# The masked constant on VectorE, normalising passes in halves, scores one column block per slot

## The chip, the cores and the metric

The kernel runs on one core of a Trainium2 chip. A core has TensorE (matmuls into eight PSUM banks; PE in the profile, its weight loads PEld), VectorE (DVE), ScalarE (ACT), GpSimd (POOL), and SyncE (SP), which here issues the DMA transfers. The metric is device time in microseconds, the median of several executions.

## The reference, cut to what matters

Graph attention over 128 graphs of 128 nodes with 768 features, 12 heads of 64, in float32:

```python
h = jnp.maximum(_layernorm(x, axis=-1), 0.0)
q = split_heads(h @ Wq + bq); k = split_heads(h @ Wk + bk); v = split_heads(h @ Wv + bv)
scores = einsum('bhqd,bhkd->bhqk', q, k) / sqrt(64)
scores = scores + beta * adj[:, None]
scores = where(adj[:, None] > 0, scores, -9000000000000000.0)
probs = softmax(scores, axis=-1)
out = einsum('bhqk,bhkd->bhqd', probs, v)
x = x + merge_heads(out)
```

## The kernel before, in words

The graphs are taken in 32 groups G of four. A round of the main loop works on one group in three slices: `qk0` (queries and keys of the first six heads), `v` (values of all heads) and `qk1` (queries and keys of the other six). Every slice multiplies the same activations by other weights with a fast matrix product of fifteen block products in four chains. Each chain adds up in PSUM, and the sum is read out after each product that finishes something. So a later product of a chain has to wait until the earlier state has been read. One product is one **slot**; slots 0 to 14 run in the order `ZORDER`.

In `qk0` and `v` a product is once more cut into seven zones (`product_z`, matmuls L495), in two banks of four and three zones. Its activation operand needs four sums made by GpSimd (`inner`, L418 to L421), its weights come ready-made from DRAM as a tile `T` (L297, a ring of five). After the product its result goes to a tile of queries/keys or values. The first product that touches a tile **opens** it with copies: in `qk0` four by ScalarE (L514 to L517), in `v` two by VectorE with the bias (L508, L510) and two by ScalarE (L509, L511). Later products are added by VectorE (L521 for the first bank, L522 for the second). When a tile is whole, GpSimd recombines the zones (`decode`, L540 to L543 for queries and keys, L551 to L556 for values). In slice `qk0` slot 6 opens a tile from the two banks of chain a, and slot 8 is the next product of that chain; slice `v` is laid out alike. Slice `qk1` uses plain products (L571, L581, L587).

Into these slots other work is woven by the tables `todo`: a step under `at` is issued after the slot's matmuls and before its read-out, one under `(at, "post")` behind the read-out. Inside this region the order written is the order on each engine, so an engine that stands at one instruction holds up all that is queued behind it. The woven steps that matter here:

- `scores` (L609): the scores of column blocks of two heads, into two banks each; VectorE adds the bias tile and caps them (L613), ScalarE takes the exponential (L616). The first half of the heads is done in slots 1 and 2 of slice `v`: two column blocks (2, 0) in slot 1, the third (1) in slot 2.
- `norm` (L400): ReLU, scale and shift of a graph of the next group on ScalarE, four passes of 128x192 in place; slots 0, 2, 4 and 6 of slice `v`. `to_hT` (L406) transposes the result on VectorE.
- `bias_steps` (L436 to L449): makes the bias tile `biasT` of the next group, in slots 3, 5, 6 and 12 of slice `qk0`. In slot 5 GpSimd fills it with the masked constant (L439) and VectorE makes the predicate `kp` (L441) and the scaled adjacency (L442); in slot 6 VectorE copies the adjacency over the constant where the predicate says so (L444), and ScalarE squares the adjacency for a check of ranges (L445).
- `attend`: probabilities times values (L646), divided by the row sums (L623 to L630), added to the input by GpSimd (L656) and stored.

The first groups are handled by a separate start-up; rounds G = 2 to 30 have the bias steps in slice `qk0`, rounds G = 1 to 30 the normalising passes in slice `v`.

Of the kernel before, what the change touches and what calls it, by code (L numbers as in the profile page):

```python
# [19 lines left out]
GRP = 4  # L20
EPS = 1e-5
MASKED = -9000000000000000.0
# [92 lines left out]
def direct(ctx, tc, x, adj, wq, bq, wk, bk, wv, bv, beta, out, bad):  # L115
# [10 lines left out]
    nc = tc.nc  # L126
# [10 lines left out]
    NB = P // SQ  # L137
# [14 lines left out]
    def home_x(G, g):  # L152
        if not g % 2:
            xp[G, g // 2] = work.tile([P, 2 * NB, QD], F32, tag="x", name=f"x_{G}_{g}", bufs=2)
        t = xg[G, g] = xp[G, g // 2][:, (g % 2) * NB:(g % 2 + 1) * NB, :]
        return t
# [9 lines left out]
    for g in range(2):  # L166
        t = home_x(0, g)
# [158 lines left out]
    def moments_1(G, lo, hi):  # L326

        n = hi - lo
        bank = pm[G, lo, "bank"] = take()
        pm[G, lo] = bank[:, 0:4 * n].rearrange("p (s b h) -> p s b h", s=2, h=2)  # L330
        for q in range(0, P, HD):
            nc.tensor.matmul(pm[G, lo][q:q + HD, 0], mean8.rearrange("p a i -> p (a i)")[:, q:q + HD],
                             halves(G, lo, hi, 1), start=True, stop=True)
        mean = stat.tile([P, n], F32, tag="mean", name=f"mean_{G}_{lo}", bufs=2)
        nc.vector.tensor_reduce(mean, pm[G, lo][:, 0], AX.X, ALU.add)
        d = stat.tile([P, n, 2], F32, tag="dev", name=f"dev_{G}_{lo}", bufs=2)
        nc.vector.tensor_tensor(d, halves(G, lo, hi, 1), mean[:, :, None].to_broadcast([P, n, 2]), ALU.add)
        nc.vector.tensor_tensor(d, d, d, ALU.mult)
        nc.vector.scalar_tensor_tensor(d, halves(G, lo, hi, 2), 2.0 / QD, d, op0=ALU.mult, op1=ALU.add)
        return mean, d  # L340

    def moments_2(G, lo, hi, mean, d):

        n = hi - lo
        for q in range(0, P, HD):
            nc.tensor.matmul(pm[G, lo][q:q + HD, 1], mean8.rearrange("p a i -> p (a i)")[:, q:q + HD], d,
                             start=True, stop=True)
        ve = stat.tile([P, n], F32, tag="ve", name=f"ve_{G}_{lo}", bufs=2)
        nc.vector.tensor_reduce(ve, pm[G, lo][:, 1], AX.X, ALU.add)
        give(pm[G, lo, "bank"])  # L350
        nc.vector.tensor_scalar(ve, ve, -1.0, EPS, op0=ALU.mult, op1=ALU.add)
        r = stat.tile([P, n], F32, tag="rstd", name=f"rstd_{G}_{lo}", bufs=2)
        nc.gpsimd.tensor_tensor(r, ve, nhalf.to_broadcast([P, n]), ALU.pow)
        t = stat.tile([P, n], F32, tag="shift", name=f"shift_{G}_{lo}", bufs=2)
        shifted = nc.gpsimd.tensor_tensor(t, mean, r, ALU.mult)
        for b in range(lo, hi):
            rstd[G, b], shift[G, b] = r[:, b - lo:b - lo + 1], t[:, b - lo:b - lo + 1]
        return shifted
# [34 lines left out]
            for b in range(NB):  # L393
                rstd[G, g * NB + b], shift[G, g * NB + b] = to[:, b, 0, g:g + 1], to[:, b, 1, g:g + 1]

    def norm(G, g):
        for b in range(NB):
            t = xg[G, g][:, b, :]
            n = g * NB + b
            nc.scalar.activation(t, t, AF.Relu, bias=shift[G, n], scale=rstd[G, n])  # L400
# [32 lines left out]
    def bias_steps(G):  # L433

        a = turned[G] = work.tile([P, GRP, N], F32, tag="adjT", name=f"adjT_{G}", bufs=1)
        nc.vector.transpose(a, turned.pop((G, "raw")).rearrange("p g b j -> p g (b j)"))  # L436
        yield
        t = biasT[G] = work.tile([P, GRP, N], F32, tag="biasT", name=f"biasT_{G}", bufs=2)
        nc.gpsimd.memset(t, MASKED)  # L439
        kp = work.tile([P, GRP, N], U8, tag="kp", name=f"kp_{G}", bufs=1)  # L440
        nc.vector.tensor_scalar(kp, a, 0.0, None, op0=ALU.is_gt)  # L441
        nc.vector.tensor_scalar(a, a, beta_c, BIAS_CAP * ISCALE, op0=ALU.mult, op1=ALU.min)  # L442
        yield
        nc.vector.copy_predicated(t, kp, a)  # L444
        nc.scalar.activation(a, a, AF.Square, scale=1.0005 * math.sqrt(SUM_CAP) / (BIAS_CAP * ISCALE))  # L445
        yield
        bm = stat.tile([P, GRP], F32, tag="bm", name=f"bm_{G}", bufs=1)
        nc.vector.tensor_reduce(bm, a, AX.X, ALU.max)
        nc.vector.tensor_tensor(seen[:, 16:20], seen[:, 16:20], bm, ALU.max)  # L449
# [305 lines left out]
    def slice_of(G, sl, todo, order=range(len(PRODUCTS))):  # L755
        run([product(G, sl, n, order) for n in order], todo)

    def slice_z(G, sl, todo):
        run([product_z(G, sl, n) for n in ZORDER], todo)
# [167 lines left out]
    def then(at, f, *args):  # L927
        todo.setdefault(at, []).append(lambda: f(*args))

    def bias(G, *at):  # L930
        def go():
            if G not in steps:
                steps[G] = bias_steps(G)
            next(steps[G], None)
        for n in at:
            then(n, go)

    def attention(G, u, at):
        for i, j in enumerate((2, 0, 1)):
            then(at[i] - 3, load_xo, G, 3 * u + j)  # L940
            then((at[i], "post"), attend, G, 3 * u + j)

    def at_slots(f, G, slots):
        for at, names in slots:
            for name in names:
                then(at, f, G, *((int(name[1]), int(name[2])) if f is to_hT else (name,)))

    def activations(G):

        at_slots(to_hT, G, ((2, ("A10",)), (9, ("A12",))))  # L950
        at_slots(sum_acts, G, ((2, (0,)), (3, (2,)), (5, (3,)), (6, (4,)), (7, (5,)), (10, (1,)), (11, (6,)), (12, (7,)),
                               (13, (8,)), (14, (9,))))
        at_slots(inner, G, ((6, (0,)), (7, (4,)), (8, (2,)), (9, (1,)), (10, (8,)), (11, (6,)), (12, (5,)), (13, (3,)),
                            (14, (10,))))

    def rest_of_activations(G):
        at_slots(sum_acts, G, ((0, (10,)),))
        at_slots(inner, G, ((0, (7,)), (1, (13,)), (2, (9,)), (3, (11,)), (4, (12,)), (5, (14,))))
# [48 lines left out]
    for G in range(1, NG):  # L1007
        more = G + 1 < NG
        todo.clear()
        if G > 1:  # L1010
            rest_of_activations(G)
        else:
            at_slots(to_hT, 1, ((0, ("A00",)),))
            at_slots(sum_acts, 1, ((0, (2,)), (1, (5,)), (2, (4,)), (3, (8,)), (5, (9,))))
            at_slots(inner, 1, ((0, (2,)), (1, (6,)), (2, (5,)), (3, (10,)), (4, (7,)), (5, (13,)), (6, (9,)), (7, (14,))))
        for n, order in ((1, (2, 0)), (2, (1,))):
            then((n, "post"), scores, G - 1, 1, order)
        attention(G - 1, 1, AV_Z)
        if G == 1:
            bias(1, 0, 2, 3, 5)  # L1020
            for r in range(2):
                then(r, load_x, 2, r)
            for g in range(GRP):
                then(5 + 2 * g, stats, 2, g)
            then(6, add_raw, 2)
            then(13, lambda: mom.extend(moments_1(2, 0, GRP * NB)))
            then(14, lambda: moments_2(2, 0, GRP * NB, *mom[2:]))
        elif more:
            bias(G + 1, 3, 5, 6, 12)
        slice_z(G, "qk0", todo)  # L1030

        todo.clear()
        for n, order in ((1, (2, 0)), (2, (1,))):
            then((n, "post"), scores, G, 0, order)
        if more:
            for g in range(GRP):
                then((0, 2, 4, 6)[g], norm, G + 1, g)
            for name, at in (("A01", 4), ("A00", 5), ("A02", 6), ("A11", 9)):
                then(at, to_hT, G + 1, int(name[1]), int(name[2]))
            if G == 1:  # L1040
                bias(2, 8, 9, 10, 12)
                for at, n in enumerate((3, 4, 5, 6, 7, 8, 9, 10, 13, 14)):
                    then(at + 3, sum_weights, "qk1", n)
            if G + 2 < NG:
                then(13, load_halves, G + 2, 0)
        slice_z(G, "v", todo)
        if not more:
            break

        todo.clear()  # L1050
        attention(G, 0, AV_AT)
        activations(G + 1)
        if G + 2 < NG:
            for g, at in enumerate((2, 5, 8, 11)):
                then(at, row_stats, G + 2, g)
                if g < 3:
                    then(at, load_halves, G + 2, g + 1)
            for r, at in enumerate((6, 11)):
                then(at, load_x, G + 2, r)
            then(13, row_moments, G + 2)  # L1060
            then(14, add_raw, G + 2)
        slice_of(G, "qk1", todo)
# [154 lines left out]
```

## Time and profile before

| what | value |
|---|---|
| median of three runs | 2959.27 us (2958.37 to 2959.87) |
| the profiled execution's own time | 2957.3 us |
| its span | 2955.5 us |
| mean granted TensorE clock | 0.981 |
| DMA traffic | 660.88 MB, mean 224 GB/s |

A round takes 89.3 us in the trace. A line of a timeline gives the start and the length in us, the engine, the source line, the operation, what it writes and reads, its shapes, how many such instructions follow each other, and in brackets how long the engine was idle before it and for what it waited. An instruction may start before the one ahead of it on its engine has ended. A matmul of float32 shows as two records of 64 columns of weights. A line of the waits gives who waited, for whom, the total in us, how often, and the longest. A line of the windows gives the stretch, its length, the busy time and instructions of PE, PEld, DVE, ACT and POOL, the granted clock, the DMA share and GB/s.

### The profile page before, as it was taken

The numbers are of one execution on the slowest core, as the hardware profiler recorded it, in microseconds if no ns is written. First come the engines' busy times: TensorE is split into PE (matmuls) and PEld (weight loads), VectorE is DVE, ScalarE is ACT, GpSimd is POOL, SyncE is SP. The second block draws the span as 40 slices with busy tenths as digits, with TensorE's granted clock in tenths as the row PEclk, the third lists the DMA queues.
The fourth block names the chain that finished last, engine by engine and source line by source line (L and its number), as shares of the span: only waits on it lengthen the run. The fifth ranks groups of instructions, "written<-read, shape, count | busy, mean of one in ns | idle before, by whom it ended". The sixth has DMA issues, their size and how long they took to land.

```text
span 2955.5 us, 113446 instructions
## 1 busy us (share of the span) xinstructions
PE 2784.0 (94%) x46433; PEld 2431.7 (82%) x46433; DVE 2131.3 (72%) x4794; ACT 1351.1 (46%) x3999; POOL 2287.8 (77%) x4086
## 2 busy tenths in 40 slices
PE   7989999999999999999999999999999999999998
PEld 6778888888888888888888788888888887888887
DVE  3877777677777777777777776777777777767765
ACT  1435444445344444444454444444444544444443
POOL 2777878777877778887878877788877787777883
PEclk9999999999999999999999999999999999999999
DMA  9678777877777777778777777777787777777764
GB/s 216 196 236 232 217 218 229 244 236 215 219 236 219 248 230 217 218 226 247 235 221 215 233 220 246 232 213 226 224 244 236 218 216 230 225 242 230 212 193 130
DMA packets 526217, 660.88 MB, mean 224 GB/s; under 512 B 105460, under 2 KB 401664, under 8 KB 525696
## 3 DMA queue, kind: packets, MB, share of 16 engines
q1 hardware_dynamic: 525368, 653.20, 75.1%
q8 instruction: 368, 6.03, 0.8%
q14 instruction: 153, 1.25, 0.1%
q10 hardware_dynamic: 328, 0.40, 0.1%
HBM read 589.26 MB, written 64.21 MB: 221 GB/s over the span
## 4 chain that ended last, share of the span: by engine, by line


## 5 line engine op out<-in xcount | busy, mean ns | idle before, releaser
L495 PE MATMUL bank<-spbuf,T_qk 128*64 128x128 f32 x7440 | 673.3, 278 | 0.2 <-issue 0.2
L630 ACT ACTIVATE o<-bank,sm 128x64 f32<-128x64 f32 x1524 | 354.8, 315 | 667.9 <-DVE sm L624 522.8
L495 PE MATMUL bank<-T_v,spbuf 128*64 128x128 f32 x7440 | 647.8, 273 | 0.0
L646 PEld LDWEIGHTS bank<-v,e 128*64 128x64 f32 x6048 | 434.8, 144 | 107.5 <-ACT o L630 0.2
L495 PE MATMUL bank<-S,T_qk 128*64 128x128 f32 x4092 | 414.9, 282 | 109.7 <-ACT qk L515 106.3
L495 PEld LDWEIGHTS bank<-T_v,spbuf 128*64 128x64 f32 x7440 | 458.4, 137 | 0.3 <-ACT o L630 0.3
L646 PE MATMUL bank<-v,e 128*64 128x65 f32 x6048 | 449.4, 228 | 0.0
L495 PEld LDWEIGHTS bank<-spbuf,T_qk 128*64 128x64 f32 x7440 | 445.4, 141 | 0.5 <-issue 0.5
L495 PE MATMUL bank<-T_v,S 128*64 128x128 f32 x4092 | 402.8, 275 | 17.5 <-ACT v L509 15.6
L581 ACT ACTIVATE qk<-bank,bqk 128x256 f32<-128x256 f32 x372 | 156.7, 475 | 551.6 <-PE bank L571 422.0
L571 PE MATMUL bank<-S,wqk 128*64 128x256 f32 x2976 | 389.5, 380 | 0.0
L495 PEld LDWEIGHTS bank<-S,T_qk 128*64 128x64 f32 x4092 | 252.9, 142 | 127.0 <-ACT qk L515 113.5
L521 DVE TENSOR_TENSOR v<-v,bank 128x512 f32<-128x512 f32 x310 | 211.9, 684 | 150.4 <-PE bank L495 96.6
L571 PE MATMUL bank<-S,qk_T 128*64 128x256 f32 x2480 | 305.6, 379 | 0.0
L551 POOL TENSOR_TENSOR v<-v 128x128 f32<-128x128 f32 x186 | 86.0, 462 | 269.4 <-ACT x L400 145.2
L656 POOL TENSOR_TENSOR xo<-xo,o 128x512 f32<-128x512 f32 x189 | 242.7, 1284 | 57.0 <-ACT o L630 57.0
L613 DVE SCALAR_TENSOR_TENSOR e<-bank,biasT 128x512 f32<-128x512 f32 x378 | 237.4, 683 | 67.9 <-PE bank L609 67.7
L495 PEld LDWEIGHTS bank<-T_v,S 128*64 128x64 f32 x4092 | 257.1, 137 | 30.8 <-ACT v L509 23.3
L587 DVE TENSOR_TENSOR qk<-qk,bank 128x512 f32<-128x512 f32 (+1 forms) x311 | 208.2, 670 | 47.3 <-PE bank L571 34.0
L521 DVE TENSOR_TENSOR qk<-qk,bank 128x512 f32<-128x512 f32 x310 | 210.7, 680 | 42.8 <-ACT qk L515 22.7
L616 ACT ACTIVATE e<-e 128x512 f32<-128x512 f32 x378 | 227.3, 629 | 17.8 <-DVE e L613 17.3
L540 POOL TENSOR_TENSOR qk<-qk 128x256 f32<-128x256 f32 x186 | 135.7, 730 | 106.3 <-DVE qk L521 58.4
(164 smaller groups left out, 5883.2 us busy)
## 6 DMA issues: line engine op xcount, KB each, us to landing
T_qk<-kept_qk SPq DMA_DIRECT2D x465, 448.0 KB, 4.6
T_v<-kept_v SPq DMA_DIRECT2D x465, 448.0 KB, 4.9
x<-in_x_dram SPq DMA_DIRECT2D x254, 192.0 KB, 4.7
xo<-in_x_dram SPq DMA_DIRECT2D x189, 256.0 KB, 4.8
out_dram<-xo SPq DMA_DIRECT2D x189, 256.0 KB, 5.2
half<-in_x_dram SPq DMA_DIRECT2D x232, 192.0 KB, 4.0
adj<-in_adj_dram SPq DMA_DIRECT2D x128, 64.0 KB, 2.6
kept_qk<-prep_qk SPq DMA_DIRECT2D x15, 448.0 KB, 5.0
```

What stands on the lines that cost most here:

```text
L495: nc.tensor.matmul(p[z // 4][q:q + HD, z % 4, :], lhs[:, q:q + HD], rhs, start=(first and z % 4 == 0), stop=True, skip_group_check=True)
L521: nc.vector.tensor_tensor(t[:, 0:4], t[:, 0:4], p[0], op)
L540: e.tensor_tensor(t[:, 1:4:2], t[:, 1:4:2], twice(0), ALU.add)
L551: e.tensor_tensor(v[:, 0:2, 0:HD], heads(0), heads(3), ALU.add)
L571: nc.tensor.matmul(p[q:q + HD, i, :], lhs[:, q:q + HD], rhs, start=(first and i == 0 and c == 0), stop=(c == 1), skip_group_check=True)
L581: opened[0] = nc.scalar.activation(t[:, i, :], p[:, i, :], AF.Identity, bias=bqk[:, i, oc:oc + 1], scale=float(sign))
L587: added[G] = nc.vector.tensor_tensor(t[:, :, cols], t[:, :, cols], p[:, :, cols], ALU.add if sign > 0 else ALU.subtract)
L613: taken[0] = nc.vector.scalar_tensor_tensor(e, ps[oc, i].rearrange("p (g n) -> p g n", g=GRP), SCORE_CAP * ISCALE, biasT[G], op0=ALU.min, ...
L616: nc.scalar.activation(e, e, AF.Exp, scale=1.0 / ISCALE)
L630: nc.scalar.activation(o[:, b], pa[:, b, 0:HD], AF.Copy, scale=t[:, 1, b:b + 1])
L646: nc.tensor.matmul(pa[q:q + HD, 2 * g + i, :], es[G, oc, i][:, 2 * r + g, q:q + HD], vt[G, "v", r, h // 4][:, 4 * g + h % 4, :], start=Tru ...
L656: nc.gpsimd.tensor_add(t, t, o.rearrange("p a (b j) d -> p (a b) (j d)", j=2))
```

## The change

Three edits, which change no arithmetic:

1. The memset that fills `biasT` with the masked constant is issued to VectorE instead of GpSimd, at the same place in the program.
2. In slice `v` the four passes of the first two graphs' `norm` are issued in halves, two passes behind the read-out of each of slots 0 to 3; those of the third and fourth graph go to slots 4 and 5 (before the read-out, where they were in 4 and 6). Three of the transposes `to_hT` come one slot later.
3. The scores in slice `v` are done one column block in each of slots 1, 2 and 3, in the order 2, 0, 1.

```diff
-    def norm(G, g):
-        for b in range(NB):
+    def norm(G, g, lo=0, hi=NB):
+        for b in range(lo, hi):
             t = xg[G, g][:, b, :]
             n = g * NB + b
             nc.scalar.activation(t, t, AF.Relu, bias=shift[G, n], scale=rstd[G, n])
...
         t = biasT[G] = work.tile([P, GRP, N], F32, tag="biasT", name=f"biasT_{G}", bufs=2)
-        nc.gpsimd.memset(t, MASKED)
+        nc.vector.memset(t, MASKED)
...
         todo.clear()
-        for n, order in ((1, (2, 0)), (2, (1,))):
+        for n, order in ((1, (2,)), (2, (0,)), (3, (1,))):
             then((n, "post"), scores, G, 0, order)
         if more:
-            for g in range(GRP):
-                then((0, 2, 4, 6)[g], norm, G + 1, g)
-            for name, at in (("A01", 4), ("A00", 5), ("A02", 6), ("A11", 9)):
+            for g in range(2):
+                for h in range(2):
+                    then((2 * g + h, "post"), norm, G + 1, g, 2 * h, 2 * h + 2)
+            for g in range(2, GRP):
+                then(2 + g, norm, G + 1, g)
+            for name, at in (("A01", 5), ("A00", 6), ("A02", 7), ("A11", 9)):
                 then(at, to_hT, G + 1, int(name[1]), int(name[2]))
```

## The prediction

> **What bounds the kernel now.** I read the page's first section, then the page's groups, the waits sorted by total, and last the timelines of one round (one group of four graphs), engine by engine. The rounds repeat closely, so one stands for the rest.
>
> ```profile
> span 2955.5 us, 113446 instructions
> PE 2784.0 (94%) x46433; PEld 2431.7 (82%) x46433; DVE 2131.3 (72%) x4794; ACT 1351.1 (46%) x3999; POOL 2287.8 (77%) x4086
> ```
>
> TensorE is the bound, and only 2955.5 − 2784.0 = 171.5 us of its time is idle. Whoever wants to be faster without touching the matmuls has to find this idle time. The waits name it:
>
> ```profile
> ACT adjT L445 <- DVE biasT L444: 144.7, 31, 7.4
> DVE biasT L444 <- POOL biasT L439: 126.5, 29, 4.4
> PE bank L495 <- ACT qk L515: 106.3, 29, 3.7
> PE bank L495 <- ACT v L509: 15.6, 29, 1.1
> PE bank L609 <- POOL qk L543: 6.0, 19, 0.4
> ```
>
> The columns are who waited, for whom, us in total, times, longest. One wait, 29 times 3.67 us, holds 106.3 of the 171.5 us: matmuls of slice qk0 wait for an opening copy of ScalarE. The two lines above it occur as often and have the same size: ScalarE's L445 waits for VectorE's L444, which waits for GpSimd's memset L439. The timelines of GpSimd, VectorE, ScalarE and TensorE show whether they are one chain:
>
> ```profile
> 1425.26 0.53 POOL L439 MEMSET biasT<- 128x512 f32 x1
> 1427.27 0.73 POOL L540 TENSOR_TENSOR qk<-qk 128x256 f32<-128x256 f32 x1 [1.48 <-ACT adjT L445]
> ...
> 1420.22 0.65 DVE L441 TENSOR_SCALAR kp<-adjT 128x512 uint8<-128x512 f32 x1
> 1420.90 0.56 DVE L442 TENSOR_SCALAR adjT<-adjT,beta_c 128x512 f32<-128x512 f32 x1
> 1425.82 0.73 DVE L444 COPY_PREDICATED biasT<-kp,adjT 128x512 f32<-128x512 uint8 x1 [4.35 <-POOL biasT L439]
> ...
> 1421.49 0.36 ACT L517 ACTIVATE qk<-bank,bqk 128x128 f32<-128x128 f32 x1
> 1426.58 0.63 ACT L445 ACTIVATE adjT<-adjT 128x512 f32<-128x512 f32 x1 [4.73 <-DVE biasT L444]
> 1427.12 0.35 ACT L514 ACTIVATE qk<-bank,bqk 128x128 f32<-128x128 f32 x1
> 1427.37 0.48 ACT L515 ACTIVATE qk<-bank 128x384 f32<-128x384 f32 x1
> ...
> 1423.61 0.39 PE L495 MATMUL bank<-S,T_qk 128*64 128x128 f32 x4
> 1423.83 0.39 PE L495 MATMUL bank<-spbuf,T_qk 128*64 128x128 f32 x4
> 1427.90 0.44 PE L495 MATMUL bank<-S,T_qk 128*64 128x128 f32 x4 [3.69 <-ACT qk L515]
> ```
>
> They are. The memset stands in GpSimd's queue behind its zone sums and ends at 1425.79. VectorE had all else for L444 at 1421.46 and starts it at 1425.82, 0.03 us behind the memset. ScalarE stands 4.73 us at L445, and behind it in its queue are the copies L514 to L517 that empty slot 6's two banks. Slot 8 adds onto those banks, so TensorE starts it at 1427.90, 0.05 us after L515 ends, where the step between starts (1423.83 − 1423.61 = 0.22) would have given 1424.05. The hole is 3.85 us from start to start.
>
> **Part 1, the memset on VectorE.** It leaves GpSimd's queue and stands on VectorE ahead of L441. No row shows a VectorE memset of 128x512. Below it costs nothing but an issue; above, the 0.73 of L444, which reads two tiles and writes one of this size. I take 0.56, L442's row, one pass over the same shape. Then L441, L442 and L444 follow without a wait, and L444 starts at 1421.46 + 0.56 = 1422.02, 3.80 earlier. What is queued behind the memset on VectorE is only L441, L442 and L444 themselves. ScalarE is free from 1421.85 (end of L517), so L445 also comes 3.80 earlier, at 1422.78, L514 at 1423.32, and L515 ends at 1427.85 − 3.80 = 1424.05. Slot 8 could start at 1424.10, against 1424.05 by TensorE's own pace. So 0.05 us of the hole is left, 3.80 goes. With 0.73 it would leave 0.22, with nothing it would leave none and TensorE itself limits: the gain lies between 3.6 and 3.85 a round. 29 rounds give −110 us (−105 to −112).
>
> The Trainium skill prices it: "VectorE: DVE Perf Modes", section on zero memsets issued as uint32, has a memset take one cycle per element whatever the type, which at the page's 0.96 GHz is an estimated 0.53 us; the sum by that is less than 1 us away. No run here shows it yet.
>
> What is late next? GpSimd keeps its backlog of zone sums (the last ends at 1425.26, where the memset began, and belongs to slot 14, six products on) and then the decodes L540 to L543. These now start at 1425.26 rather than 1427.27, 2.0 us earlier where TensorE is 3.8 us earlier. At the end of that queue scores wait for L543 already (6.0 us over 19 times). Without idle GpSimd gains back the 1.48 us before L540 and smaller gaps, and in part 3 the third column's scores move one product later, so I put nothing for it; it costs up to 0.4 a round if that is wrong.
>
> **Part 2, V's opening copies and the normalising passes.** ScalarE is the tight engine in the first seven slots of slice v:
>
> ```profile
> 1442.81 1.86 ACT L400 ACTIVATE x<-x,block 128x192 f32<-128x192 f32 x4
> 1444.56 0.49 ACT L509 ACTIVATE v<-bank 128x384 f32<-128x384 f32 x1
> 1446.53 0.49 ACT L509 ACTIVATE v<-bank 128x384 f32<-128x384 f32 x1 [1.20 <-DVE v L508]
> 1447.27 2.42 ACT L616 ACTIVATE e<-e 128x512 f32<-128x512 f32 x4
> 1451.99 1.14 ACT L616 ACTIVATE e<-e 128x512 f32<-128x512 f32 x2
> 1457.91 0.48 ACT L509 ACTIVATE v<-bank 128x384 f32<-128x384 f32 x1
> ...
> 1443.09 0.28 DVE L508 TENSOR_TENSOR v<-bv_b,bank 128x128 f32<-128x128 f32 x1
> 1445.08 0.69 DVE L521 TENSOR_TENSOR v<-v,bank 128x512 f32<-128x512 f32 x1 [1.52 <-ACT v L509]
> 1446.55 2.48 DVE L613 SCALAR_TENSOR_TENSOR e<-bank,biasT 128x512 f32<-128x512 f32 x4
> ...
> 1444.61 1.98 PE L609 MATMUL bank<-qk 64*64 64x128 f32 x64
> 1446.52 0.44 PE L495 MATMUL bank<-T_v,S 128*64 128x128 f32 x4
> 1449.68 0.45 PE L609 MATMUL bank<-qk 64*64 64x128 f32 x8 [0.36 <-POOL qk L543]
> 1458.44 0.44 PE L495 MATMUL bank<-T_v,S 128*64 128x128 f32 x4 [0.52 <-ACT v L509]
> ```
>
> From 1442.81 to slot 6's copy at 1457.91 it runs through, but for 1.20 us; slot 8 waits for that copy (0.52). The change keeps every one of these instructions ahead of slot 6's copy: four graphs' passes, five pairs of copies, six exponentials. So it can only shift ScalarE's idle time. Four shifts. First, it starts with L509 instead of the norm, which waits for L508: 1443.09 + 0.28, and 0.10 for the signal, is 1443.47, +0.66. Second, L521 of slot 1, which stood 1.52 us for the late L509 (0.49 from 1444.56), needs L509 (now 1443.47 + 0.49 = 1443.96) and slot 1's matmuls, done at the latest when the scores start at 1444.61: it comes 0.5 to 1.0 us sooner, and with it slot 1's L508 and L509, at 1445.5 to 1446.0. ScalarE is ready for that at 1443.47 + 0.77 (a pair of copies: 1446.53 − 1.20 − 1444.56) + 0.93 (half a norm of 1.86) = 1445.17; its idle is 0.35 to 0.85 instead of 1.20, on the mean −0.6. Third, the first column's exponentials follow slot 1's copies at once, and their L613 starts only when that column's scores end: 0 to 0.3 of new idle, +0.15. Fourth, three pairs of exponentials (3 × 1.14) against four and two (2.42 + 1.14), −0.14. Together about +0.1 a round, with ends −0.5 (slot 8's wait of 0.52 gone) and +0.6 (the second shift does not come): over 30 rounds +3 us, from −15 to +18.
>
> **Part 3, one column of scores per slot.** Same matmuls (64 in 1446.52 − 1444.61 = 1.91, 0.96 a column), spread over three slots. It lets go the wait for L543 in the last column (0.36). But slot 8 is held by ScalarE, which isn't sooner, so TensorE just waits there longer: 0 us. Every L613 keeps its duration; VectorE and ScalarE get the pairs in the order that they had. Three transposes L406 come one slot later on VectorE, the first right behind the last half pass, ahead of slot 5's L508; they feed slice qk1, which starts nine slots on, and VectorE waits there for ScalarE as it does now: 0. No DMA, and no queue of GpSimd or SyncE, is moved by parts 2 and 3.
>
> **The sum.** 2957.3 us is the profiled execution's own time (span 2955.5), 2.0 below the median of the runs shown, 2959.27. 2957.3 − 110 + 3 = 2850; against the median 2852. About 0.2% (6 us) is what a measurement of this kernel can tell from no change.
>
> **Rivals.** *DMA becomes the next wait.* The hole was also time in which T tiles caught up:
>
> ```profile
> 1424.20:1427.90 3.70, 0.02 (x2) 0.00 (x0) 1.76 (x3) 1.32 (x4) 2.22 (x5) 1.00 1.04 359
> 1427.90:1441.40 13.50, 13.50 (x292) 13.50 (x294) 10.72 (x29) 5.13 (x22) 11.21 (x16) 1.00 0.75 232
> 1458.40:1469.20 10.80, 10.76 (x198) 10.76 (x199) 8.28 (x15) 0.26 (x1) 10.17 (x22) 1.00 0.88 307
> ```
>
> The last two columns are the DMA share and GB/s. 359 × 3.7 + 232 × 13.5 = 4.46 MB now pass in 17.2 us and must pass in 13.4. At 359 GB/s that takes 12.4 us and hides; at the 307 of the end of slice v, where products also follow each other without a hole and TensorE hardly waits, 14.5, 1.1 us a round too much: 29 × 1.1 = 32, so 2884. For it: DMA is full in the hole. Against it: five tiles of lead, and only the last bytes of the stage must be in time. 0.12. The Trainium skill, "DMA: Bandwidth & Descriptors", Specifications, gives some 358 GB/s as the limit of HBM for one core; the trace agrees (359), so there is little above the demand of 333 GB/s.
>
> *V's first slots cost more* (the upper end of part 2): 2867. 0.12.
>
> *Slower: V's slots 1 to 3 begin to alternate.* With one column per slot ScalarE might stand for each column's scores (0.96) and its first L613 (0.62 each of the 2.48), 1.58 three times, and 0.66 at the start, less the 1.20 there is now: 4.2 a round. Over 3.8 it eats part 1; here it would end at +0.4 × 30 = +12, 2971. It decides from the point at which ScalarE has emptied its queue before a column's scores end. Against it: ScalarE still owes two passes when the second and third columns arrive. 0.03.
>
> *The change doesn't do what it says*: L444 waits for something else that ends at the same time. 0.03 us after the memset, in 29 rounds, speaks against it. 2959, 0.04.
>
> **How the numbers follow.** Forecast 0.69 (2835 to 2867, parts 1 and 2 with their ends), DMA 0.12, V worse 0.12, none 0.04, slower 0.03. The range takes in the forecast's ends and reaches to the DMA case: 2835 to 2884. Faster 0.93, same 0.04, slower 0.03.
>
> **What would show it.** Right: the wait for L515 falls below 10 us in total, L444's wait for L439 is gone, the wait for L509 grows from 15.6 to some 30 or 40 us (the slots before it run undisturbed, ScalarE no faster), a VectorE memset of about 0.56 us appears 32 times. Wrong: matmuls L495 waiting for DMA T_qk by more than 10 us, waits for POOL L543 grown, or the wait for L509 above 60 us.

## The result and the profile after

| | median us | lowest to highest | ratio to before, 95% interval |
|---|---|---|---|
| before, beside it | 2959.57 | 2958.37 to 2961.78 | |
| after | 2828.45 | 2826.57 to 2829.16 | 0.9555 [0.9539, 0.9572] |

The change makes the kernel 131 us faster. Forecast were 2852 us, in a range that began at 2835. The sign holds, but the time is 23.5 us under the forecast and lies below the range.

The first section of the page after:

```profile
span 2827.0 us, 113416 instructions
PE 2753.4 (97%) x46433; PEld 2391.0 (85%) x46433; DVE 2187.4 (77%) x4826; ACT 1357.7 (48%) x3999; POOL 2293.8 (81%) x4054
```

TensorE's idle time went from 171.5 to 2827.0 − 2753.4 = 73.6 us, 97.9 less. But the span is 128.5 shorter: TensorE's *busy* time fell as well, by 30.6 us, with the same 46433 instructions. The prediction had looked for time in the idle part alone, and had taken the busy part as fixed.

Every ratio in this document is to the kernel before, run beside the kernel in question; the median of before was 2951.5 to 2959.6 us in the four batches of runs.

The waits after (who, for whom, us in total, times, longest), then the groups by line:

```profile
ACT adjT L445 <- DVE biasT L444: 32.2, 31, 7.7
PE bank L495 <- ACT v L509: 35.4, 30, 1.2
PE bank L495 <- DMA T_qk<-kept_qk: 3.6, 2, 3.0
PE bank L609 <- POOL qk L543: 0.7, 2, 0.4
```
```profile
L444 DVE COPY_PREDICATED biasT<-kp,adjT 128x512 f32<-128x512 uint8 x32 | 28.0, 874 | 1.0
L439 DVE MEMSET biasT<- 128x512 f32 x32 | 15.5, 485 | 1.8
L441 DVE TENSOR_SCALAR kp<-adjT 128x512 uint8<-128x512 f32 x32 | 11.6, 363 | 0.0
```

The wait for L515 (106.3 us) and L444's wait for L439 (126.5) are gone; the wait for L509 has grown from 15.6 to 35.4; DMA is no new wait. The same place as in the prediction's timelines, in one round of after, on VectorE, ScalarE and TensorE:

```profile
1363.35 0.55 DVE L522 TENSOR_TENSOR qk<-qk,bank 128x384 f32<-128x384 f32 x1
1363.96 0.48 DVE L439 MEMSET biasT<- 128x512 f32 x1
1364.36 0.36 DVE L441 TENSOR_SCALAR kp<-adjT 128x512 uint8<-128x512 f32 x1
1364.76 0.56 DVE L442 TENSOR_SCALAR adjT<-adjT,beta_c 128x512 f32<-128x512 f32 x1
1365.35 0.88 DVE L444 COPY_PREDICATED biasT<-kp,adjT 128x512 f32<-128x512 uint8 x1
...
1366.26 0.63 ACT L445 ACTIVATE adjT<-adjT 128x512 f32<-128x512 f32 x1 [0.81 <-DVE biasT L444]
1366.80 0.35 ACT L514 ACTIVATE qk<-bank,bqk 128x128 f32<-128x128 f32 x1
1367.05 0.48 ACT L515 ACTIVATE qk<-bank 128x384 f32<-128x384 f32 x1
...
1367.43 0.39 PE L495 MATMUL bank<-spbuf,T_qk 128*64 128x128 f32 x4
1367.65 0.39 PE L495 MATMUL bank<-S,T_qk 128*64 128x128 f32 x4
```

The four VectorE instructions follow each other without a wait. L515 ends at 1367.53, and slot 8 starts at 1367.65, 0.22 behind the matmuls before it: TensorE's own step, no hole.

**Where the other 30 us were.** What the prediction did not look at is the granted clock behind the hole of the kernel before. Windows of before, at a hole (1513.53 to 1517.22) of another round than the one that the prediction quotes; columns as there, the granted clock is the third number from the end:

```profile
1513.40:1517.20 3.80, 0.13 (x4) 0.00 (x0) 1.76 (x3) 1.30 (x4) 2.33 (x5) 1.00 1.02 360
1517.20:1520.70 3.50, 3.48 (x52) 3.48 (x54) 1.10 (x4) 1.33 (x6) 2.02 (x5) 0.62 0.25 91
```

Behind the quoted hole, at 1427.90, the same stretch looks like this, and in after, behind slot 8's start, like the second fence:

```profile
1427.90:1431.40 3.50, 3.50 (x79) 3.50 (x80) 1.79 (x7) 1.41 (x6) 2.50 (x5) 1.00 0.40 131
```
```profile
1367.60:1371.10 3.50, 3.50 (x84) 3.50 (x82) 2.65 (x7) 1.40 (x6) 3.34 (x7) 1.00 1.03 347
```

Busy is 3.48 to 3.50 us in all three, but 52 matmuls pass at a clock of 0.62 and 79 or 84 at full clock. The timeline of TensorE in before shows the switch inside it:

```profile
1517.60 0.39 PE L495 MATMUL bank<-spbuf,T_qk 128*64 128x128 f32 x4
...
1517.94 0.53 PE L495 MATMUL bank<-spbuf,T_qk 128*64 128x128 f32 x4
1518.25 0.44 PE L646 MATMUL bank<-v,e 128*64 128x65 f32 x4
1518.47 0.65 PE L495 MATMUL bank<-S,T_qk 128*64 128x128 f32 x4
```

Four matmuls of one form take 0.39, then 0.65 us. In the trace's record of the clock this is a stretch of 3.41 us at half clock, and it stands behind 22 of the 29 holes of before (behind one more it is 6.83 long). In after there is none in the rounds from G = 2 on. The mean times of a round's parts, worked out from the starts of the first matmuls of the slots, over the undisturbed middle of each trace, in us (before is split by the clock):

```
kernel                       rounds  qk0 0-8  qk0 8-end  v 0-2  v 2-8  v 8-end   qk1   round
before, full clock                5    19.32      13.55   5.06  11.91    10.84  28.70   89.38
before, 3.41 at half clock       21    19.31      15.12   5.06  11.39    10.75  28.70   90.32
before, all                      26    19.31      14.81   5.06  11.49    10.77  28.70   90.14
after                            26    15.47      13.69   4.19  12.95    10.75  28.70   85.75
memset_only                      27    15.49      13.68   5.89  11.41    10.79  28.70   85.96
without_memset                   26    19.30      16.27   4.19  12.94    10.75  28.70   92.15
columns_only                     26    19.27      14.43   4.19  12.37    10.75  28.70   89.70
memset_and_halves                25    15.47      13.65   5.90  12.66    10.75  28.70   87.14
memset_and_columns               26    15.47      13.67   4.20  12.79    10.75  28.70   85.58
late_by_4                        27    18.02      14.13   4.19  12.93    10.75  28.70   88.73
late_by_7                        26    19.79      15.81   4.19  12.93    10.75  28.70   92.17
late_by_10                       26    21.79      15.56   4.19  12.93    10.75  28.70   93.92
norms_behind_slot6               26    15.48      13.66   4.19  11.61    10.78  28.70   84.43
```

The half clock costs 15.12 − 13.55 = 1.57 us behind the hole, of which 0.52 come back in slice v (11.91 to 11.39, since ScalarE and GpSimd are less late there: slot 2, which stops for L543, takes 3.53 to 3.56 us in the rounds at full clock and 2.71 to 3.42 in the others), and 0.94 in the round. One of the five rounds at full clock lost 0.43 us for another reason at the end of slice `v`; the other four take 89.29, against which half clock costs 1.03 a round. The kernels below the first four lines are those of the experiments.

### The profile page after: what moved, and what is told of

It reads as the page before. It is cut to its first block, busy times and chain, and to the rows that moved or that the text cites. A ratio compares the mean times of both kernels' runs of the same rounds, so it can differ in the third digit from the quotient of the medians.

```text
span 2827.0 us, 113416 instructions
## 1 busy us (share of the span) xinstructions
PE 2753.4 (97%) x46433; PEld 2391.0 (85%) x46433; DVE 2187.4 (77%) x4826; ACT 1357.7 (48%) x3999; POOL 2293.8 (81%) x4054
## 4 chain that ended last, share of the span: by engine, by line
## 5 line engine op out<-in xcount | busy, mean ns | idle before, releaser
L495 PE MATMUL bank<-spbuf,T_qk 128*64 128x128 f32 x7440 | 658.7, 273 | 0.9 <-POOL qk L543 0.5
L646 PEld LDWEIGHTS bank<-v,e 128*64 128x64 f32 x6048 | 412.3, 137 | 110.6 <-ACT o L630 0.2
L495 PEld LDWEIGHTS bank<-spbuf,T_qk 128*64 128x64 f32 x7440 | 439.2, 137 | 1.4 <-POOL qk L543 0.8
L495 PE MATMUL bank<-T_v,S 128*64 128x128 f32 x4092 | 403.3, 274 | 36.0 <-ACT v L509 35.4
L646 PE MATMUL bank<-v,e 128*64 128x65 f32 x6048 | 433.8, 221 | 0.1
L495 PE MATMUL bank<-S,T_qk 128*64 128x128 f32 x4092 | 401.5, 274 | 4.2 <-DMA T_qk<-kept_qk 3.0
L613 DVE SCALAR_TENSOR_TENSOR e<-bank,biasT 128x512 f32<-128x512 f32 x378 | 240.5, 685 | 89.4 <-PE bank L609 89.3
L418 POOL TENSOR_TENSOR spbuf<-S 128x128 f32<-128x128 f32 x341 | 182.9, 537 | 44.1 <-DVE S L411 44.1
```

The lines of the kernel that those rows point to most:

```text
L418: e.tensor_tensor(t[:, 0], a[:, 0, N:H2], a[:, 1, N:H2], ALU.add)
L495: nc.tensor.matmul(p[z // 4][q:q + HD, z % 4, :], lhs[:, q:q + HD], rhs, start=(first and z % 4 == 0), stop=True, skip_group_check=True)
L613: taken[0] = nc.vector.scalar_tensor_tensor(e, ps[oc, i].rearrange("p (g n) -> p g n", g=GRP), SCORE_CAP * ISCALE, biasT[G], op0=ALU.min, ...
L646: nc.tensor.matmul(pa[q:q + HD, 2 * g + i, :], es[G, oc, i][:, 2 * r + g, q:q + HD], vt[G, "v", r, h // 4][:, 4 * g + h % 4, :], start=Tru ...
```

## The experiments

**One edit alone, and one undone.** The theory was that the memset is all of the gain; the rival, that parts 2 and 3 carry some of it. Four kernels; the first is the kernel before with the first edit only:

```diff
-        nc.gpsimd.memset(t, MASKED)
+        nc.vector.memset(t, MASKED)
```

> Only the memset goes to VectorE; slice v as before. Theory A (the memset carries everything: it takes away the 3.85 us hole in 29 rounds, and with the hole the stretches of half clock behind it, 24 of 3.41 us in the trace of before and none in the rounds after): 2820 to 2835 us, clock 1.00 in every round, slot 8 of slice v held for 0.5 to 0.7 us. Rival B (the 23 us beyond the forecast come from slice v): 2848 to 2856 us.

Measured: 2832.29 us, 0.9584 [0.9568, 0.9600], beside 0.9555 [0.9539, 0.9572] for the whole change. The memset alone is (nearly) the whole gain; the other two edits add some 6 us (0.21 a round by the table) to 9 us (by the ratios, whose intervals overlap, so this is at the edge of what the runs can tell). What hinders it is another wait than expected, GpSimd's decode, which stopped scores 19 times for 0.3 us before:

```profile
PE bank L609 <- POOL qk L543: 20.7, 59, 0.4
```

The second undoes the first edit in the change:

> Halves and columns as in the change, the memset stays on GpSimd. Theory A: the hole and the half clock stay, slice v is 0.1 to 0.3 us a round longer: 2957 to 2970 us, 20 to 26 stretches of half clock. Rival B: 2930 to 2940 us.

Measured: 3010.88 us, 1.0183 [1.0166, 1.0200]. Both theories miss by 40 us or more. The waits (L515 106.1, L509 34.7) are the known ones and cannot explain a kernel 54 us slower than before. The table can: slice v costs 17.13, about before's 16.97 at full clock, but `qk0 8-end` costs 16.27. Two stretches behind one hole (3.65 us of idle time, up to 1361.28):

```profile
1361.30:1366.90 5.60, 5.60 (x68) 5.60 (x70) 1.82 (x6) 1.39 (x6) 2.94 (x6) 0.50 0.17 56
1366.90:1370.00 3.10, 3.10 (x71) 3.10 (x70) 1.94 (x6) 0.93 (x4) 2.90 (x4) 0.99 0.69 206
```

68 matmuls in 5.6 us, then 71 in 3.1. Here 28 of 29 holes have 6.83 us at half clock behind them, though the hole itself is before's. The reading of before above followed from this run.

The third is the memset and the halves, with the scores as before:

```diff
-        for n, order in ((1, (2,)), (2, (0,)), (3, (1,))):
+        for n, order in ((1, (2, 0)), (2, (1,))):
```

> Memset on VectorE and the normalising passes in halves; the scores as before, two columns in slot 1. Theory A: 2820 to 2840, within 10 us of the change. Rival B, if the halves are what shortens slice v: 2826 to 2830 with memset_only near 2850.

Measured: 2867.84 us, 0.9703 [0.9687, 0.9719], 28 us above the expectation's upper end. Both waits stand side by side, and ScalarE stands for L613 ahead of the exponentials (the timeline of ScalarE behind them), which is the prediction's alternating rival in small:

```profile
PE bank L495 <- ACT v L509: 34.8, 30, 1.2
PE bank L609 <- POOL qk L543: 20.2, 57, 0.4
```
```profile
1318.10 1.23 ACT L616 ACTIVATE e<-e 128x512 f32<-128x512 f32 x2 [0.49 <-DVE e L613]
...
1321.73 1.23 ACT L616 ACTIVATE e<-e 128x512 f32<-128x512 f32 x2 [0.89 <-DVE e L613]
```

The fourth is the memset and the columns, with the passes as before (slots 0, 2, 4, 6):

> Memset on VectorE and one column of scores per slot; the normalising passes as before in slots 0, 2, 4, 6. Theory A: 2820 to 2840, within 10 us of the change; waits for L543 near 0. Rival B, if the columns are what shortens slice v: 2826 to 2830 with memset_only near 2850.

Measured: 2822.33 us, 0.9550 [0.9534, 0.9566], the same as the whole change. So the halves bring nothing beside the columns. No wait of matmuls for L543 is left in this trace: the columns take them away.

**The hole alone, in three sizes.** To test the clock apart from everything else, VectorE writes the same constant several times more, in the changed kernel: 4, 7 and 10 more memsets.

```diff
-        nc.vector.memset(t, MASKED)
+        for _ in range(5):
+            nc.vector.memset(t, MASKED)
```

> The change with four more VectorE memsets of the same tile behind the first (the result is the same; each costs some 0.42 us from start to start), so that slot 8 of slice qk0 waits again, by a hole of about 1.6 us in 29 rounds. Theory A (the clock is lost only by a hole near 3.4 us): 2828 + 29 x 1.6 = 2875 us, 2865 to 2885, no stretch of half clock in the rounds. Rival C (the 24 stretches of half clock in before have nothing to do with the hole): some 20 stretches whatever its length.

Measured: 2919.02 us, 0.9888 [0.9869, 0.9908], above the expected range, as are the other two of this set. One reason is the same for all three: the memsets of one tile wait for each other and start 0.66 us apart, not 0.42, so slot 8 comes 2.55, 4.32 and 6.32 us later than in after, where 1.6, 2.9 and 4.1 were expected. VectorE in late_by_4:

```profile
1495.36 0.48 DVE L440 MEMSET biasT<- 128x512 f32 x1
1496.02 0.48 DVE L440 MEMSET biasT<- 128x512 f32 x1 [0.17 <-DVE biasT L440]
```

Waits for the copy (L516 here, one line later) are 69.0 us in 29. The round is 2.55 longer at slot 8; 29 × 2.55 = 74 and 2828 + 74 = 2902, so some 17 us more are lost. Windows over two holes of this kernel, of the same length:

```profile
1409.50:1412.00 2.50, 0.13 (x4) 0.02 (x2) 2.12 (x4) 1.34 (x4) 2.45 (x4) 0.93 1.00 329
1412.00:1415.00 3.00, 3.00 (x36) 3.00 (x38) 0.13 (x1) 0.46 (x2) 1.97 (x4) 0.50 0.82 290
1499.10:1501.60 2.50, 0.12 (x5) 0.01 (x2) 2.13 (x4) 1.33 (x4) 2.44 (x4) 1.00 1.04 363
1501.60:1504.60 3.00, 3.00 (x70) 3.00 (x72) 1.33 (x5) 1.38 (x6) 2.00 (x5) 1.00 0.62 220
```

36 against 70 matmuls in 3.00 us. Ten of the 27 middle rounds have the stretch, and they take 89.72 us where the other 17 take 88.14: 1.58 each, 16 us, which closes the sum. So a hole of 2.4 us of idle time (69.0 / 29) is long enough, but not each time, and the idea that only holes near 3.4 us matter falls.

> Seven more memsets: a hole of about 2.9 us. Theory A: 2828 + 29 x 2.9 = 2912, 2900 to 2930, no or few stretches of half clock. Rival D (a hole of any length costs clock in proportion): 2925 to 2945 and half clock in two rounds of three.

Measured: 3017.86 us, 1.0223 [1.0203, 1.0244]; all 29 holes have 6.83 us at half clock behind them. By the table 29 × (19.79 − 15.47) = 125 us are the later slot 8 and 29 × (15.81 − 13.69) = 61 the clock: 2828 + 186 = 3014.

> Ten more memsets: a hole of about 4.1 us, on VectorE's account and with GpSimd's memset gone. Theory A: 2828 + 29 x 4.1 = 2947, and on top 1 to 2.9 us for a stretch of half clock in nearly every round: 2970 to 3035. Rival C or a loss by the hole alone: 2940 to 2952.

Measured: 3071.69 us, 1.0406 [1.0385, 1.0426]; all 29 holes have a stretch at half clock behind them, 28 of 6.83 us and one of 10.24. By the table the later slot 8 is 29 × (21.79 − 15.47) = 183 us and the clock 29 × (15.56 − 13.69) = 54: 2828 + 237 = 3065.

What decides? The stretches start on a grid of 3.413 us that runs through the whole trace of each kernel without drift. Each kernel's rounds from G = 2 on, laid out on this grid, give for each grid window the share that TensorE stood idle:

```
kernel               windows that half clock follows:   windows at full clock with none
                     number, smallest idle share        behind them: largest idle share
before                    23   0.596                             0.589
late_by_4                 11   0.597                             0.590
columns_only              16   0.597                             0.592
without_memset            29   0.690                             0.374
late_by_7                 29   0.600                             0.261
late_by_10                29   0.665                             0.450
the other seven            0                                     0.354
```

Half clock follows where TensorE stood still for 0.60 of one window, some 2.0 us, in each of 137 cases, and never below. A hole of 2.4 us passes that only if it lies mostly in one window (11 of 29 in late_by_4). A hole of 3.7 us often does, but can lie across two windows so that neither reaches it (23 of 29 do in before, 16 of 29 in columns_only). A window at half clock that is itself idle for 0.23 or more is followed by another at half clock (89 cases), one idle for 0.18 or less by full clock (137).

**The wait that came up.** In after, slot 8 of slice v waits for L509 in every round. TensorE and ScalarE there:

```profile
1398.45 0.44 PE L495 MATMUL bank<-T_v,S 128*64 128x128 f32 x4 [1.18 <-ACT v L509]
```
```profile
1392.90 4.49 ACT L400 ACTIVATE x<-x,block 128x192 f32<-128x192 f32 x10
1397.29 0.47 ACT L509 ACTIVATE v<-bank 128x384 f32<-128x384 f32 x1
...
1397.92 0.48 ACT L509 ACTIVATE v<-bank 128x384 f32<-128x384 f32 x1
```

Ten passes stand ahead of the copies of slots 4 and 6, which came only at 1397.29 and 1397.92. The passes of the last two graphs are needed later than that, so they can stand behind slot 6's copy:

```diff
-                then(2 + g, norm, G + 1, g)
-            for name, at in (("A01", 5), ("A00", 6), ("A02", 7), ("A11", 9)):
+                then((4 + g, "post"), norm, G + 1, g)
+            for name, at in (("A01", 5), ("A00", 6), ("A02", 7), ("A11", 11)):
```

> The change with the passes of the third and fourth graph moved from slots 4 and 5 to behind the read-outs of slots 6 and 7, and the transpose A11 from slot 9 to 11. If ScalarE's queue ahead of slot 6's copy is what holds slot 8 of slice v (35.4 us in total), that wait goes: 2828 - 30 x 1.2 = 2793 us, 2788 to 2800, waits for L509 below 5 us. If something else is late right behind it: 2810 to 2828.

Measured: **2786.72 us**, 0.9441 [0.9425, 0.9456], faster than both kernels, and a little more than expected. Waits for L509 are 0.3 us in total, `v 2-8` went from 12.95 to 11.61, and no wait of TensorE in the rounds is left among the first lines of its waits, which now belong to the start-up and the end:

```profile
PE bank L332 <- DVE st L321: 11.4, 2, 11.1
PE bank L779 <- DVE A L406: 6.9, 1, 6.9
PE bank L495 <- DVE v L521: 5.1, 5, 3.5
```

Then the same without halves, the four passes whole in slots 0, 2 and behind slots 6 and 7:

```diff
-                then((0, 2, 4, 6)[g], norm, G + 1, g)
-            for name, at in (("A01", 4), ("A00", 5), ("A02", 6), ("A11", 9)):
+                then((0, 2, (6, "post"), (7, "post"))[g], norm, G + 1, g)
+            for name, at in (("A01", 4), ("A00", 5), ("A02", 6), ("A11", 11)):
```

> The memset on VectorE and one column block of scores per slot, but no half passes: the normalising passes whole, in slots 0 and 2 ahead of the read-out, and behind the read-out of slots 6 and 7. If what counts in slice v is only that the last two graphs' passes stand behind slot 6's copy, the halves are not needed: 2786 us (2782 to 2791), a round of 84.3 us, no wait of matmuls for L509 over 5 us in total. If the halves are what lets slot 1's and slot 2's copies come early, it is slower than that by 0.3 us or more a round, 2795 us or more, with waits for L609's banks or L509 back.

Measured: 2788.57 us, 0.9436 [0.9421, 0.9452]: the halves are not needed.

And that kernel with the scores in two columns and one, as before:

> As the kernel before it, but the scores stay as two column blocks in slot 1 and one in slot 2. The columns' own theory: the wait of the third column's matmuls for GpSimd's L543 stays, some 20 us in total, and the wait for L509 is gone: 2786 + 20 = 2806 us (2798 to 2812). If instead the scores' order doesn't matter once the passes are behind slot 6, it is within 5 us of 2786.

Measured: 2833.21 us, 0.9592 [0.9576, 0.9608]. The columns matter, but by 45 us, not 20. The waits are as expected; the timeline of TensorE shows why they are too small a measure:

```profile
PE bank L609 <- POOL qk L543: 20.2, 58, 0.4
```
```profile
1386.70 1.58 PE L609 MATMUL bank<-qk 64*64 64x128 f32 x40
1388.64 0.89 PE L609 MATMUL bank<-qk 64*64 64x128 f32 x24 [0.36 <-POOL qk L543]
1389.45 0.44 PE L495 MATMUL bank<-T_v,S 128*64 128x128 f32 x4
```

From the first score to the next product 1389.45 − 1386.70 = 2.75 us pass, where the undisturbed pair of columns that the prediction shows took 1.91. The stop is called 0.36 and costs 0.84: the ends of matmuls in flight are modelled, and the idle time counts only from there. There are two such stops a round. By the starts of the slots, slots 1 to 3 of slice v together take 9.60 us here and 8.08 with one column each, and 29 × 1.52 = 44 of the 45 us. In memset_and_halves the same three slots take 9.59, which accounts for its 1.4 us a round above the whole change.

Last, the columns alone, with the memset on GpSimd:

> One column block of scores per slot alone, memset on GpSimd, passes as before. By the waits it takes some 0.3 us a round from the kernel before (89.3 to 89.0 without half clock), that is 2930 us; on top comes the half clock behind the hole of 3.7 us. If stretches of 3.41 us at half clock follow in most rounds, as in the kernel before, 2945 to 2960. If the rounds lock to 27 windows of 3.413 us (92.15 us), as with halves and columns together, two windows at half clock follow in every round and it is 3000 to 3015. If neither clock effect is there, 2930.

Measured: 2940.66 us, 0.9953 [0.9936, 0.9970], 4 us under the nearest range. Its rounds at full clock take 88.97 us, 0.41 less than before's five with 89.38 and 0.32 less than the undisturbed four with 89.29; 0.3 was expected. Half clock follows 16 of its holes, fewer than in before; 13 middle rounds with one window take 1.28 us more, one with two 2.47 more, 19 us. Before with its 22 us of half clock taken out would be 2953.6 − 22 = 2932; 29 × 0.41 = 12 less and 19 of its own make 2939. The hole and its wait (105.3 us) are those of before; that fewer of its holes reach the 0.60 is a matter of phase, and luck.

## Why the prediction was right in its sign and too small

*The bound and the chain.* Right: L515, L444 and L439 were one chain. The hole went by 19.31 − 15.47 = 3.84 us, forecast 3.80. The memset took 0.485 us where 0.56 was chosen from L442's row; the estimate of 0.53 from the Trainium skill, "VectorE: DVE Perf Modes", lay nearer, and 0.485 is still a little below it. L441 fell from 0.65 in the quoted row to 0.36, L444 rose from 0.73 to 0.88; why wasn't tried.

*"Slot 8 could start ... by TensorE's own pace", and "the rounds repeat closely, so one stands for the rest".* This is the step that failed: the hole was priced by its idle time alone, 3.80 a round, and the sum has no term for the clock behind it. The rounds do not repeat in the granted clock, and the 89.3 us that was given for a round is that of the rounds at full clock; the mean is 90.14. The quoted round happened to be one of 6 in 29 whose hole is followed by full clock; in the others TensorE ran at half clock for 3.41 us, and that went with the hole. Against rounds at full clock the change is worth 89.38 − 85.75 = 3.63 us, 29 × 3.63 = 105 (103 by the undisturbed four), which is the forecast's 107. Against the mean round it is 90.14 − 85.75 = 4.39, 127. The difference, 0.76 × 29 = 22 us, is nearly all of the miss of 23.5. It could have been read: the mean granted clock of 0.981 was in the table, and the page of before has the loads of weights at two prices:

```profile
L646 PEld LDWEIGHTS bank<-v,e 128*64 128x64 f32 x6048 | 434.8, 144 | 107.5 <-ACT o L630 0.2
L495 PEld LDWEIGHTS bank<-T_v,spbuf 128*64 128x64 f32 x7440 | 458.4, 137 | 0.3 <-ACT o L630 0.3
```

Many of the first stand right behind the hole, none of the second do; in after both take 137 ns. The Trainium skill has the rule, "TensorE: Matmul & The Clock Gate", Part 1: a free-running window of some 3.4 us, half clock after an idle window. The prediction did not weigh it. The runs agree on the grid (3.413 us), but not on the idle time: 0.60 of a window was enough.

*What is late next on GpSimd* was put at nothing, at most 0.4 a round. Alone, the memset does bring it: L543 stops scores 59 times instead of 19, and slice v's first eight slots cost 17.30 instead of 16.97. In the change the columns take it away, as part 3 said of the last column.

*Part 2*, forecast +0.1 a round from −0.5 to +0.6: slots 0 to 8 of slice v went from 16.97 (full clock) to 17.14, +0.17. Right in sum, and in part by luck, since its pieces were off and cancelled. In the round of after that is shown, which begins slice v at 1381.32, ScalarE starts 0.86 later against the slice than in the quoted round of before (forecast 0.66), its idle time shrinks from 1.20 to 0.33 (−0.87, forecast −0.6), and a pair of exponentials takes 1.23, not 1.14. *Part 3*, forecast 0 because ScalarE holds slot 8 anyway. Parts 2 and 3 cannot be priced one by one: beside the memset alone (0.9584) the halves alone cost 35 us (0.9703), the columns alone bring 10 (0.9550), both together 9 (0.9555). The halves need the columns, not the other way round, and what the columns bring is the wait for L543.

*The signs to look for* came as listed: L515 gone, L444's wait for L439 gone, L509 at 35.4 (30 to 40), 32 memsets, no DMA wait above 10 us. They could not tell 2852 from 2828, since all of them are waits, and the missing term was no wait. The range was added up wrongly too: the ends of parts 1 and 2 give 2832 to 2872, not 2835 to 2867. The measured time lies below both.

*Rivals.* DMA: not met, 3.6 us in two waits, though the core moves 347 GB/s in the place of the hole, near the 359 of the hole that the prediction shows. The mean rose from 224 to 234 GB/s. V's slots 1 to 3 alternating: not in the change; seen in memset_and_halves as 0.49 and 0.89 a round.

## What to carry to other kernels

A stall of TensorE can cost more than its idle time: look at the granted clock in a window right behind it, in many rounds and not in one, and price a hole that goes with the half clock that goes with it. Compare busy time at equal instruction counts: if the same matmuls are busy longer in one kernel, the clock is the reason to check first. And an edit that moves nothing in the waits can still change the time when it shifts the phase of a periodic hole against the clock's grid.

## What the runs showed of the hardware

- Half clock follows after an idle share of 0.60 of one grid window of 3.413 us, some 2.0 us: behind all 137 windows of 0.596 or more, in six kernels, and behind none of 0.592 or less, in thirteen. It ends behind a window that is idle for 0.18 or less and goes on behind one of 0.23 or more.
- A periodic kernel can lock to the grid: the rounds of without_memset take 92.15 us and those of late_by_7 92.17, which is 27 windows (27 × 3.413 = 92.16), though their holes differ by 0.5 us; each then meets the same half clock in every round. That is how undoing an edit worth 3.84 us a round cost 6.4. The traces show the phase settle there: the rounds of late_by_7 from G = 2 on take 92.50, 92.34, 92.26, 92.21, 92.18, 92.18 and then 92.16 us. In late_by_10 they come to alternate between 93.33 and 94.41, and two of them are 55 windows (187.73).
- A short stop in the middle of matmuls, 0.36 us by the waits, cost 0.84 from start to start.
- Memsets of one tile on VectorE took 0.485 us each and started 0.66 us apart.
